# A two-layer graph block on one core: a unit's last sums stay in their PSUM banks, the edge weights are clipped on ScalarE, the maxima are spread in a line buffer

## The chip, the core and the metric

The kernel runs on one core of a Trainium2 chip. The metric is the device time in microseconds of one launch; the kernel before takes 1951.85 us (median of three runs, 1951.63 to 1953.33). One profiled execution has a span of 1949.7 us. The engines are named as in the profile: PE (TensorE, with PEld for its weight loads), DVE (VectorE), ACT (ScalarE), POOL (GpSimd) and SP (SyncE); the last two issue most of the DMAs here.

## The reference, cut to what matters

There are 4096 nodes with 512 features, and a symmetric pattern `adj` of 4096 x 4096 with positive weights on about 1.6% of the places.

```
# layer 0
x  = layernorm(x + relu(adj @ (max(sign(x), 0) @ sign(w0).T)))
# layer 1
node_att = softmax(x @ node_w, axis=0)
h = x @ edge_w
e = where(adj > 0, h @ h.T, -9e15)
out = (adj * node_att * softmax(e, axis=1)) @ (x @ w1) + bias
x  = layernorm(x + out)
```

## The kernel before, in words

The kernel has four stages in order of time.

1. 0 to about 950 us: layer 0. `adj` is split into two parts (`hi`, `lo`), and both are multiplied with the small integers of the other operand (L372, L373). The normalised rows go to DRAM, both as they are (`x1_d`) and in the combinations that later products need (`lop_d`).
2. `h`, transposed, in seven products for each 2 x 2 of blocks (`seven`, L100).
3. To about 1078 us: the scores. Blocks of 512 x 512 of `h @ h.T` are computed once each (`Single` L632, `Couple` L701) and turned for their mirror image (L602, L603). Each row block gets its mask and its row maximum on DVE (L564) and its sum of exponentials on ACT (L573). The raw scores go to DRAM (`s_d`).
4. From 1078 us to the end: the aggregation, which the change touches. It is a loop over 16 *units*, `Aggregate(g, r)` with g = 0..3 outside and r = 0..3 inside. A unit takes four score blocks: destinations g and g + 4, sources r and r + 4. DVE subtracts the row maximum (`shift`, L815), ACT takes the exponential (L816), and DVE multiplies by the edge weights, which are first clipped at zero (`weigh`, four instructions of 128 x 512 in L822). From the four blocks `r11, r12, r21, r22`, DVE makes the four combinations of a seven-product scheme in place (`combine`, L831 to L839: `t3`, then `t1`, `t2`, `t4`). PE multiplies seven pairs (index `m` in `main`): `m=0` is `r11`, 1 is `r21`, 2 is `r22`, 3 is `t4`, 4 is `t1`, 5 is `t2`, 6 is `t3`. Each product has two *halves* of one PSUM bank, four 128 x 512 matmuls in fp32, which the trace shows as eight passes (L991). A half is then read out of its bank into `total`, the sums over r: by an ACT copy at r = 0 (L995), by a DVE add at r > 0 (L997). From unit 2 to unit 14 product 0 is itself cut into seven smaller ones that are laid between the others (`second`, L932).

When the four units of one g are done, `todo` brings `join` (L1024) and `Finish`: a product with `w1` (L1079, read by DVE in L1090), the layernorm (L1120 to L1133), and the output.

What sets the order: one unit's `steps()`, the work that prepares the *next* unit (loads, masks, `shift`, `weigh`, `combine`), are dealt out evenly over the halves of the present one by `between`. Work of the first unit is `early_steps`, mixed into the end of stage 3. The tile framework then orders the instructions of each engine by its own estimates, so they can stand in another order than in the code; an engine takes its instructions in that order. Waits are on semaphores.

Buffers: `free` holds 6 + 7 tiles of 128 x 2048 (`slot`, `lent`), taken and given back in turn; `free_e` holds six lines of 128 x 512 (`line`); `rows` is a pool of four tiles of 128 x 512, which the `Finish` steps use for their rows `xb` (L1052, freed when the output DMA has read them) and `panel` for `spread`. Six PSUM banks go round in `next_bank`. `lopp` has four buffers for the left operands, loaded on SP's queue (L987).

`panel(A)` brings the row maxima of a destination group into a form in which they can be subtracted along the free axis: DVE spreads them (L775), PE transposes them (L781), ACT copies the result to a line (L785), which `shift` needs. It comes first in the work that a unit with r = 3 does for the next g.

Of the kernel before, what the change touches and what calls it, by code (L numbers as in the profile page):

```python
# [11 lines left out]
F32 = mybir.dt.float32  # L12
BF16 = mybir.dt.bfloat16
F32R = mybir.dt.float32r
AF = mybir.ActivationFunctionType
ALU = mybir.AluOpType
AX = mybir.AxisListType

P = 128
# [9 lines left out]
def kernel(  # L29
# [13 lines left out]
    nc = tc.nc  # L43
# [5 lines left out]
    BG = W // P  # L49
    HB = NB // 2  # L50
    HG = NG // 2
# [5 lines left out]
    rows = ctx.enter_context(tc.tile_pool(name="rows", bufs=4))  # L57
# [100 lines left out]
    with (  # L158
# [109 lines left out]
        ends = wp.tile([P, 2 * W], F32, name="ends", tag="ends")  # L268
# [74 lines left out]
        with tc.manual_schedule(engines={mybir.EngineType.DVE, mybir.EngineType.Activation}):  # L343
            for n in range(NB):
                b = n // 2 + n % 2 * HB
# [53 lines left out]
        more = [stream.tile([P, 2, 2 * W], F32, name="more", tag="stream") for _ in range(2)]  # L399
# [68 lines left out]
    free_e = deque(pan.tile([P, W], F32, name=f"line{n}", bufs=1) for n in range(6))  # L468
# [8 lines left out]
    def tick(force=False):  # L477
        now[0] += 1
        if turns and (turns[0][0] <= now[0] or force):
            turns.popleft()[1]()  # L480
        n = 1 + (len(stats) > 8)
        while stats and n and (stats[0][0]() <= now[0] or force):
            n -= stats[0][1]
            stats.popleft()[2]()
        for _ in range(1 + (len(exps) > 3)):
            if exps and (exps[0][0] <= now[0] or force):
                exps.popleft()[1]()

    def is_in(store, buf):
        return any(b is buf for b in store)  # L490

    def reclaim():

        for t, *hs in lent:
            if len(free_h) - 2 >= min(len(masks), 3) and all(is_in(free_h, h) for h in hs):
                for n in reversed(range(len(free_h))):
                    if is_in(hs, free_h[n]):
                        del free_h[n]
                free.append(t)

    def take(store=None):
        store = free if store is None else store
        while True:
            if closing[0] and store is free:
                reclaim()
            if store:
                break
            assert turns or stats or exps, (len(free), len(free_h), len(free_e), len(masks), now)
            tick(True)
        if closing[0] and store is free_h:  # L510
            for _, *hs in lent:
                if is_in(store, hs[0]) != is_in(store, hs[1]):
                    while not is_in(hs, store[0]):
                        store.rotate()
                    break
        return store.popleft()
# [236 lines left out]
    banks = deque()  # L753

    def next_bank():
        banks.rotate(-1)
        return banks[-1]
# [3 lines left out]
    def panel(A):  # L761

        cols = slice(A * BG, (A + 1) * BG)
        nm = small.tile([P, BG], F32, name="nm")
        nc.vector.tensor_reduce(nm, nmax_c[:, cols, :], AX.X, ALU.min)
        d = small.tile([P, BG, NG], F32, name="d")
        nc.vector.tensor_tensor(d, nm.unsqueeze(2).to_broadcast([P, BG, NG]), nmax_c[:, cols, :], ALU.subtract)
        nc.scalar.activation(d, d, AF.Exp)
        nc.vector.tensor_mul(d, d, sum_c[:, cols, :])
        f = pan.tile([P, BG], F32, name="f")  # L770
        nc.vector.tensor_reduce(f, d, AX.X, ALU.add)
        nc.vector.reciprocal(f, f)
        nc.vector.tensor_mul(f, f, node_att[:, cols])
        spread = rows.tile([P, BG, P], F32, name="spread", tag="rows")
        nc.vector.tensor_copy(spread, nm.unsqueeze(2).to_broadcast([P, BG, P]))  # L775
        if banks:
            pt = next_bank().rearrange("p (b w) -> p b w", w=P)
        else:
            pt = ps_tr.tile([P, BG, P], F32, name="ptm", tag="tr")
        for i in range(BG):  # L780
            nc.tensor.transpose(pt[:, i, :], spread[:, i, :], ident)  # L781
        if A % HG:
            free_e.append(panels[A - 1][1])
        mrow = take(free_e)
        nc.scalar.copy(mrow.rearrange("p (b w) -> p b w", w=P), pt)  # L785
        panels[A] = f, mrow


    pinned = [tc.keep_in_program_order]

    class Aggregate:
# [23 lines left out]
            pinned[0](nc.vector._custom_dve(TENSOR_ADD_SAT, out=q, in0=q, in1=m, s0=0.0, s1=-HUGE))  # L815
            nc.scalar.activation(q, q, AF.Exp)  # L816

        def weigh(self, n, then):
            q, a = self.q[n], self.a[n].rearrange("p b (c i) -> p b c i", i=P)
            for c in range(BG):  # L820
                qc = q[:, c, :].rearrange("p (b w) -> p b w", w=P)
                pinned[0](nc.vector.scalar_tensor_tensor(qc, a[:, :, c, :], 0.0, qc, ALU.max, ALU.mult))  # L822
            free.append(self.a[n])
            if then:
                self.mask(then)
# [15 lines left out]
        def steps(self, beside):  # L841

            self.q, self.a, self.since = [None] * 4, [None] * 4, [None] * 8

            def begin():
                for n in range(2):
                    self.load(n)
                    self.mask(n)
                if not beside:
                    self.load(2)  # L850
                    self.load(3)

            yield begin
            yield lambda: self.shift(0)
            yield lambda: self.shift(1)
            for n in range(2):
                yield lambda n=n: self.weigh(n, n + 2)
                yield lambda n=n: self.shift(n + 2)
            yield lambda: self.weigh(2, None)
            yield lambda: self.weigh(3, None)  # L860
            for n in range(4):
                yield lambda n=n: self.combine(n)

# [114 lines left out]
        def main(self, between, nxt=None, two=False):  # L978
            r11, t1, r21, r22 = self.q
            total = sums[:, self.g % 2]  # L980
            last = self.g == HG - 1 and self.r == HG - 1
            products, others = self.second(nxt) if two else ({}, {})
            turn = 0
            for m in (0, 1, 5, 6, 4, 2, 3) if last else (1, 2, 4, 6, 5, 3) if two else (0, 1, 2, 4, 6, 5, 3):
                rop = (lambda: r11, lambda: r21, lambda: r22, lambda: self.t4, lambda: t1, lambda: self.t2, lambda: self.t3)[m]()
                lop = lopp.tile([P, BG, HD], F32, name="lop")
                nc.sync.dma_start(lop, lop_d[self.r][:, m])  # L987
                for h in range(2):
                    ps = next_bank()
                    for c in range(BG):  # L990
                        nc.tensor.matmul(ps, lop[:, c, ts(h, P)], rop[:, c, :], start=(c == 0), stop=(c == BG - 1))  # L991
                    turn += 1
                    read = products[turn]() if turn in products else None
                    if self.r == 0:
                        nc.scalar.copy(total[:, m, h, :], ps)  # L995
                    else:
                        nc.vector.tensor_add(total[:, m, h, :], total[:, m, h, :], ps)  # L997
                    if read:
                        read()
                    between()  # L1000
                    if h:
                        free.append(rop)
                    for act in others.get(turn, ()):
                        act()
                if last:
                    for done in self.joins.get(m, ()):
                        join(self.g, done, nc.vector)

        joins = {1: (0,), 5: (1,), 6: (2,), 4: (3, 4), 2: (5,), 3: (6,)}

    def join(g, n, engine):

# [135 lines left out]
    def between():  # L1148
        tick()
        soon[0] = max(1, 2 - sum(m.t is not None for m in final))  # L1150
        while masks and len(free_h) > 2 and masks_h[0] < 8 and masks[0].unit <= unit[0] + 1:
            masks.popleft().load()
        for _ in range(2):
            if closing[0] and len(early_) > 2 and (len(early_) > 10 or now[0] % 2) and early_[0][0]():
                early_.popleft()[1]()
            if len(early_) < 10:
                break
# [61 lines left out]
    for n, u in enumerate(blocks):  # L1219
        nxt = blocks[n + 1] if n + 1 < len(blocks) else None  # L1220
        two = 2 <= n < len(blocks) - 1
# [5 lines left out]
        if nxt:  # L1227
            first.extend(nxt.steps(two))
            if n:
                first.popleft()()  # L1230
            if u.r == HG - 1:
                first.extendleft([lambda: panel(nxt.g + HG), lambda: panel(nxt.g)])
# [64 lines left out]
```

## Time and profile before

| engine | busy us | share of the span |
|---|---|---|
| PE | 1931.1 | 99% |
| DVE | 1438.0 | 74% |
| ACT | 694.8 | 36% |
| POOL | 300.1 | 15% |

In stage 4 the four costliest groups on DVE are the adds of L997 (148 of 680 ns, 100.6 us), the `shift` of L815 (2285 ns each for 128 x 2048), the `weigh` of L822 (684 ns each for 128 x 512) and the `combine` subtractions (2284 ns each). How to read it: a matmul row of 128 x 512 has a mean of 592 ns, but the passes overlap; in a run without waits a new pass starts each 429 ns (16 passes in 6.87 us in the chain of waits). The same holds for DVE, whose instructions start 0.60 us apart where one is listed with 0.68. Times in the timeline are microseconds from the span's start.

### The profile page before, as it was taken

What the parts mean: (1) busy time and instruction counts of PE and PEld (TensorE: products, weight loads), DVE (VectorE), ACT (ScalarE), POOL (GpSimd) and SP (SyncE); (2) the same over time, 40 slices, a digit from 0 to 9 for tenths busy, and PEclk for the clock granted to TensorE, in tenths of its full rate; (3) what the DMA queues carried; (4) which work ended last, traced back from release to release, by engine and by line L of the source; (5) the groups of instructions that cost most, each with busy time, mean ns of one, the idle gap of its engine ahead of it and who ended that gap; (6) DMA issues with size and microseconds to landing.
All of it is one profiled execution on the core that took longest, in us unless ns stands there. A gap on an engine that the chain in (4) does not pass through costs nothing.

```text
span 1949.7 us, 19192 instructions
## 1 busy us (share of the span) xinstructions
PE 1931.1 (99%) x6470; PEld 1153.5 (59%) x6470; DVE 1438.0 (74%) x2281; ACT 694.8 (36%) x1140; POOL 300.1 (15%) x424
## 2 busy tenths in 40 slices
PE   9999999999999999999999999999999999999998
PEld 6888888888644445455555444555555555555555
DVE  7766676676774576577565897898759987799757
ACT  5433333333213567577667420131303221231200
POOL 0122222122441111111121111110101110111000
PEclk9999999999999999999999999999999999999999
DMA  8888898888485578577679986776767766776731
GB/s 304 298 324 313 291 323 313 314 308 292 143 296 202 182 256 296 205 260 280 253 288 324 334 292 234 273 262 204 264 236 279 272 228 246 264 271 209 257 119 44
DMA packets 139010, 504.59 MB, mean 259 GB/s; under 512 B 14112, under 2 KB 14112, under 8 KB 131232
## 3 DMA queue, kind: packets, MB, share of 16 engines
q1 hardware_dynamic: 63648, 226.52, 34.0%
q0 software_dynamic: 66912, 247.49, 33.9%
q10 hardware_dynamic: 8352, 29.36, 4.2%
q8 instruction: 51, 0.84, 0.2%
q14 instruction: 47, 0.39, 0.1%
HBM read 381.68 MB, written 121.63 MB: 258 GB/s over the span
## 4 chain that ended last, share of the span: by engine, by line
PE 85%; DVE 5%; DMA 4%; issue 4%; ACT 1%; POOL 0%; SPq 0%; POOLq 0%; DVEq 0%; ACTq 0%
PE bank L991 29%; PE seven L701 12%; PE acc L373 11%; PE acc L372 11%; PE seven L100 5%; PE pe L632 4%; PE bank L932 3%; PE po L1079 3%; PE pt L602 2%; DMA s_d<-slot 2%; PE bank L1079 1%; PE acc L245 1%; PE pt L332 1%; PE pw L213 1%; ACT line L573 1%
## 5 line engine op out<-in xcount | busy, mean ns | idle before, releaser
L372 PE MATMUL acc<-xw,hi 128*128 128x512 f32 x960 | 376.4, 392 | 0.0
L373 PE MATMUL acc<-xw,lo 128*128 128x512 f32 x960 | 374.2, 390 | 0.0
L991 PE MATMUL bank<-lent,lop 128*128 128x512 f32 x800 | 356.2, 592 | 2.0 <-issue 1.4
L991 PE MATMUL bank<-slot,lop 128*128 128x512 f32 x784 | 349.6, 592 | 0.4 <-DMA lop<-lop_d 0.4
L991 PEld LDWEIGHTS bank<-lent,lop 128*128 128x128 f32 x800 | 151.6, 190 | 166.7 <-issue 160.8
L991 PEld LDWEIGHTS bank<-slot,lop 128*128 128x128 f32 x784 | 148.3, 190 | 161.2 <-issue 154.0
L364 DVE TENSOR_TENSOR lo<-at,hi 128x1024 fp32r<-128x1024 f32 x120 | 148.0, 1234 | 85.2 <-ACT hi L362 85.2
L373 PEld LDWEIGHTS acc<-xw,lo 128*128 128x128 f32 x960 | 180.3, 188 | 37.1 <-DVE lo L364 0.3
L372 PEld LDWEIGHTS acc<-xw,hi 128*128 128x128 f32 x960 | 180.2, 188 | 36.8
L362 ACT CAST hi<-at 128x1024 fp32r<-128x1024 f32 x120 | 126.4, 1054 | 203.4 <-PE acc L372 148.4
L997 DVE TENSOR_TENSOR over<-over,bank 128x512 f32<-128x512 f32 x148 | 100.6, 680 | 72.0 <-PE bank L991 71.9
L816 ACT ACTIVATE slot<-slot 128x2048 f32<-128x2048 f32 x37 | 70.7, 1911 | 182.0 <-DVE slot L815 160.6
L632 PE MATMUL pe<-hT 128*128 128x512 f32 (+3 forms) x384 | 132.1, 486 | 0.0
L564 DVE CUSTOM_DVE_ANT_0 line<-lent,slot 128x512 f32<-128x512 bf16 x144 | 93.0, 687 | 45.9 <-ACT slot L642 23.0
L573 ACT ACTIVATE line<-line,nmax_c 128x512 f32<-128x512 f32 x160 | 114.8, 724 | 22.2 <-DVE nmax_c L564 22.1
L816 ACT ACTIVATE lent<-lent 128x2048 f32<-128x2048 f32 x27 | 51.6, 1912 | 127.2 <-DVE lent L815 92.0
L701 PE MATMUL seven<-hT 128*128 128x512 f32 x192 | 89.8, 593 | 0.0
L815 DVE CUSTOM_DVE_ANT_1 slot<-slot,line 128x2048 f32<-128x2048 f32 x37 | 84.4, 2284 | 6.6 <-DMA slot<-s_d 5.7
L632 PEld LDWEIGHTS pe<-hT 128*128 128x128 f32 x384 | 64.6, 191 | 41.4 <-issue 33.8
L602 PEld LDWEIGHTS pt<-ident,lent 128*128 128x128 f32 x412 | 51.2, 141 | 53.0 <-issue 38.4
L1124 ACT ACTIVATE rstd<-mv,eps 128x1 f32<-128x1 f32 (+1 forms) x14 | 4.1, 296 | 213.6 <-DVE mv L1121 169.2
L603 ACT COPY slot<-pt 128x512 f32<-128x512 f32 (+3 forms) x126 | 69.5, 554 | 27.0 <-PE pt L602 23.2
(257 smaller groups left out, 2837.3 us busy)
## 6 DMA issues: line engine op xcount, KB each, us to landing
at<-in_adj_t_dram SPq DMA_DIRECT2D x60, 1024.0 KB, 6.6
lop<-lop_d SPq DMA_DIRECT2D x99, 512.0 KB, 4.8
slot<-s_d POOLq DMA_DIRECT2D x37, 1024.0 KB, 7.1
lent<-in_adj_t_dram POOLq DMA_DIRECT2D x37, 1024.0 KB, 7.5
s_d<-slot POOLq DMA_DIRECT2D x33, 1024.0 KB, 7.2
slot<-in_adj_t_dram POOLq DMA_DIRECT2D x27, 1024.0 KB, 7.3
lent<-s_d POOLq DMA_DIRECT2D x27, 1024.0 KB, 7.3
lent<-in_adj_dram SPq DMA_DIRECT2D x48, 512.0 KB, 5.3
```

What stands on the lines that cost most here:

```text
L100: nc.tensor.matmul(banks[bank][q], lop(m, q)[k], rop(m)[k], start=(first and k == 0), stop=(k == K - 1), skip_group_check=not first,)
L362: nc.scalar.copy(hi, aq)
L364: nc.vector.tensor_sub(lo, aq, hi.bitcast(F32))
L372: nc.tensor.matmul(acc, hi[:, c, :], xw[:, kb, :], start=(kb == 0), stop=False)
L373: nc.tensor.matmul(acc, lo[:, c, :], xw[:, kb, :], start=False, stop=(kb == NB - 1))
L564: nc.vector.tensor_tensor_reduce(line, mask, src, -1.0, HUGE, ALU.add, ALU.min, accum_out=nmax_c[:, b, c : c + 1])
L573: nc.scalar.activation(line, line, AF.Exp, bias=nmax_c[:, b, c : c + 1], scale=-1.0, accum_out=sum_c[:, b, c : c + 1])
L632: nc.tensor.matmul(pe[:, lo * P :], hT[:, k, ts(A * BG + i, P)], hT[:, k, (B * BG + lo) * P : (B + 1) * W], start=(k == 0), stop=(k == KD ...
L701: nc.tensor.matmul(ps, left[m][:, k, q, :], right[m][:, k, :], start=(first and k == 0), stop=(k == KD // 2 - 1), skip_group_check=not first,)
L816: nc.scalar.activation(q, q, AF.Exp)
L991: nc.tensor.matmul(ps, lop[:, c, ts(h, P)], rop[:, c, :], start=(c == 0), stop=(c == BG - 1))
L997: nc.vector.tensor_add(total[:, m, h, :], total[:, m, h, :], ps)
```

## The change: what it does and what it is for

There are four edits in stage 4.

- **Held sums.** A unit with r < 3 doesn't read out the last of its products; the two banks stay open (`held`), and the next unit begins with the same `m` and adds onto them. So that both share an `m`, the order of the products becomes 2, (0), 4, 6, 5, 3, 1 at even r and 1, (0), 4, 6, 5, 3, 2 at odd r. This is to save DVE adds.
- **Clip on ScalarE.** `max(a, 0)` leaves `weigh`: ACT applies a Relu to the weights in place (`clip`), and DVE multiplies all 128 x 2048 in one instruction. The first unit keeps the old form.
- **Spread in a line.** In stage 4 `spread` is taken from `free_e` rather than from the pool that `Finish` uses.
- The steps of a unit are laid anew so that each `clip` stands ahead of its `weigh`.

```diff
 def panel(A):
-        spread = rows.tile([P, BG, P], F32, name="spread", tag="rows")
+        if banks:
+            line = take(free_e)
+            spread = line.rearrange("p (b w) -> p b w", w=P)
+        else:
+            spread = rows.tile([P, BG, P], F32, name="spread", tag="rows")
...
         nc.scalar.copy(mrow.rearrange("p (b w) -> p b w", w=P), pt)
+        if banks:
+            free_e.append(line)
...
+        def clip(self, n):
+            nc.scalar.activation(self.a[n], self.a[n], AF.Relu)
+
-        def weigh(self, n, then):
+        def weigh(self, n, then, clipped=False):
             q, a = self.q[n], self.a[n].rearrange("p b (c i) -> p b c i", i=P)
-            for c in range(BG):
-                qc = q[:, c, :].rearrange("p (b w) -> p b w", w=P)
-                pinned[0](nc.vector.scalar_tensor_tensor(qc, a[:, :, c, :], 0.0, qc, ALU.max, ALU.mult))
+            if clipped:
+                q = q.rearrange("p c (b w) -> p c b w", w=P)
+                nc.vector.tensor_mul(q, q, a.rearrange("p b c w -> p c b w"))
+            else:
+                for c in range(BG):
+                    qc = q[:, c, :].rearrange("p (b w) -> p b w", w=P)
+                    pinned[0](nc.vector.scalar_tensor_tensor(qc, a[:, :, c, :], 0.0, qc, ALU.max, ALU.mult))
...
             yield lambda: self.shift(0)
-            yield lambda: self.shift(1)
-            for n in range(2):
-                yield lambda n=n: self.weigh(n, n + 2)
-                yield lambda n=n: self.shift(n + 2)
-            yield lambda: self.weigh(2, None)
-            yield lambda: self.weigh(3, None)
+            yield lambda: (self.shift(1), self.clip(0))
+            yield lambda: (self.weigh(0, 2, True), self.clip(1))
+            yield lambda: self.shift(2)
+            yield lambda: self.weigh(1, 3, True)
+            yield lambda: (self.shift(3), self.clip(2))
+            yield lambda: (self.weigh(2, None, True), self.clip(3))
+            yield lambda: self.weigh(3, None, True)
...
-            for m in (0, 1, 5, 6, 4, 2, 3) if last else (1, 2, 4, 6, 5, 3) if two else (0, 1, 2, 4, 6, 5, 3):
+            ends = (1, 2) if self.r % 2 else (2, 1)
+            order = (1, 0, 5, 6, 4, 2, 3) if last else (ends[0], *(() if two else (0,)), 4, 6, 5, 3, ends[1])
+            for m in order:
...
-                    ps = next_bank()
+                    more = bool(self.r) and m == order[0]
+                    keep = self.r < HG - 1 and m == order[-1]
+                    ps = Aggregate.held.pop(0) if more else next_bank()
...
-                    if self.r == 0:
+                    if keep:
+                        Aggregate.held.append(ps)
+                    elif self.r == 0 or more and self.r == 1:
                         nc.scalar.copy(total[:, m, h, :], ps)
                     else:
                         nc.vector.tensor_add(total[:, m, h, :], total[:, m, h, :], ps)
...
+        held = []
-        joins = {1: (0,), 5: (1,), 6: (2,), 4: (3, 4), 2: (5,), 3: (6,)}
+        joins = {0: (0,), 5: (1,), 6: (2,), 4: (3, 4), 2: (5,), 3: (6,)}
```

More of the change, by code (lines that the diff above doesn't have):

```diff
@@ L988, in main @@
                 for h in range(2):
-                    ps = next_bank()
+                    more = bool(self.r) and m == order[0]
+                    keep = self.r < HG - 1 and m == order[-1]
+                    ps = Aggregate.held.pop(0) if more else next_bank()
                     for c in range(BG):
-                        nc.tensor.matmul(ps, lop[:, c, ts(h, P)], rop[:, c, :], start=(c == 0), stop=(c == BG - 1))
+                        nc.tensor.matmul(
+                            ps,
+                            lop[:, c, ts(h, P)],
+                            rop[:, c, :],
+                            start=(not more and c == 0),
+                            stop=(not keep and c == BG - 1),
+                        )
                     turn += 1
                     read = products[turn]() if turn in products else None
-                    if self.r == 0:
+                    if keep:
+                        Aggregate.held.append(ps)
+                    elif self.r == 0 or more and self.r == 1:
                         nc.scalar.copy(total[:, m, h, :], ps)
```

## The prediction

> **What bounds the kernel now.** I read the page first, then PE's waits in stage 4, then single stretches of the timelines of PE, DVE and ACT.
>
> ```profile
> span 1949.7 us, 19192 instructions
> ...
> PE 1931.1 (99%) x6470; PEld 1153.5 (59%) x6470; DVE 1438.0 (74%) x2281; ACT 694.8 (36%) x1140; POOL 300.1 (15%) x424
> ```
>
> PE is the bound, and the change takes no matmul away: the passes of L991 (1584), L932 (364) and L1079 (448) stay what they are. So DVE time that is saved counts only where PE waits for DVE. How much is that in stage 4?
>
> ```profile
> PE po L1079 <- DVE left L1065: 2.4, 2, 1.2
> PE bank L991 <- issue: 1.4, 2, 0.7
> PE bank L991 <- DMA lop<-lop_d: 1.0, 2, 0.6
> ```
>
> The ends of matmuls are modelled, so these sums are somewhat too small. From the starts in PE's timeline:
>
> ```profile
> 1527.01 1.03 PE L1079 MATMUL bank<-over 128*128 128x256 f32 x4
> 1529.24 1.13 PE L1079 MATMUL po<-over,left 128*128 128x256 f32 x4 [1.20 <-DVE left L1065]
> ```
>
> Four passes of 0.216 us end at 1527.87, so the next was 1.37 late, and its first passes cost another 0.1: 1.5. Done in this way for all of stage 4, the late starts are 0.7 (at 1402.8, `lop` load), 0.2 (1473.6), 0.9 (1485.7), 1.5 (1529.2), 0.2 (1682 to 1685), 0.9 (1702.4), 1.5 (1745.9) and 0.9 (1837.1, `lop`): 6.8 us in all. That is the most the change can bring, 0.35% of the time.
>
> Where do they come from? In the timeline of DVE, at the end of g = 1:
>
> ```profile
> 1458.13 0.69 DVE L997 TENSOR_TENSOR over<-over,bank 128x512 f32<-128x512 f32 x1 [1.17 <-PE bank L991]
> 1460.01 0.43 DVE L775 COPY spread<-nm 128x512 f32<-128x512 f32 x1 [1.19 <-ACT xb L1133]
> ...
> 1462.17 0.63 DVE L775 COPY spread<-nm 128x512 f32<-128x512 f32 x1
> ...
> 1463.48 2.29 DVE L815 CUSTOM_DVE_ANT_1 slot<-slot,line 128x2048 f32<-128x2048 f32 x1 [0.23 <-ACT line L785]
> ```
>
> Unit 7 began at 1431.3, yet its first `shift` starts at 1463.5: `spread` had to wait until `Finish` let go of `rows`. Until then DVE idles 1 to 3 us before each add; after that it has a whole unit's preparation in 22 us, and is 99% busy from 1480 to 1530 (49.36 of 50 us). The lateness at 1485.7 and 1529.2, and likewise at 1702.4 and 1745.9 for g = 2, is this jam.
>
> [...]
>
> **The change part by part.**
>
> *Held sums.* Per g, the add of the last product goes away at r = 1 and 2, and the first add of r = 1 becomes an ACT copy in exchange for the one that r = 0 saves: 6 DVE adds, 24 in all, at 0.60 us apart 14.4 us of DVE. No PE time. The order of products costs something, see below.
>
> *One multiplication.* Four instructions 0.60 apart (2.41) become one of 2.28, 2.20 apart: 0.21 us saved, 60 times (15 units of 4): 12.6 us of DVE. The units beside which they stand have DVE slack, apart from the jam.
>
> *Clip.* 60 times 1.83 to 1.91 us, 110 to 115 us on ACT, which is idle most of stage 4 (9.6 of 50 us busy from 1130 to 1180). Beside PE it costs nothing in general, since six banks go round and a read-out may come some 15 us late. But `clip` adds a wait for a DMA on ACT's queue, with everything behind it waiting too. In the built order of instructions there is one place where PE is close behind: the first `clip`, of the second unit's first weights, stands at the end of stage 3, between L603 of the last full block and the last diagonal block's copies:
>
> ```profile
> 1074.01 0.59 ACT L603 COPY lent<-pt 128x512 f32<-128x512 f32 x1 [1.14 <-PE pt L602]
> 1075.36 0.72 ACT L573 ACTIVATE line<-line,nmax_c 128x512 f32<-128x512 f32 x1 [0.77 <-DVE nmax_c L564]
> ...
> 1076.08 0.46 ACT L642 COPY lent<-pe 128x384 f32<-128x384 f32 x1
> ```
>
> Those weights were issued at 1070.0 and took 6.0 us (the view of L809), so `clip` runs 1076.1 to 1077.9; L573 and the 384-wide copy follow at 1077.9 and 1078.65. PE transposes that copy:
>
> ```profile
> 1076.83 0.49 PE L602 MATMUL pt<-ident,lent 128*128 128x128 f32 x3
> 1077.15 1.06 PE L632 MATMUL pe<-hT 128*128 128x128 f32 x8
> ```
>
> Now it can start at 1079.25, 2.4 us late; the last use of `hT` ends 2.4 later, and with it the start of the `w1` load that overwrites it.
>
> *Order of products in unit 0.* Before, `t1` is the fourth product; now it is the third. The scheduler puts two of the eight 128 x 512 matmuls of `t3` ahead of it, but those need `combine(0)`.
>
> ```profile
> 1087.86 0.69 DVE L1234 TENSOR_TENSOR line<-over 128x512 f32<-128x512 f32 x1 [4.32 <-DMA over<-in_w_dram]
> ...
> 1089.99 2.49 DVE L822 SCALAR_TENSOR_TENSOR slot<-slot,slot 128x512 f32<-128x512 f32 x4
> ...
> 1093.00 2.28 DVE L831 TENSOR_TENSOR lent<-lent,slot 128x2048 f32<-128x2048 f32 x1
> 1095.32 2.29 DVE L833 TENSOR_TENSOR slot<-slot,slot 128x2048 f32<-128x2048 f32 x1
> ```
> ```profile
> 1092.11 7.03 PE L991 MATMUL bank<-lent,lop 128*128 128x512 f32 x16
> 1098.98 1.45 PE L991 MATMUL bank<-slot,lop 128*128 128x512 f32 x3
> ```
>
> DVE waits for `w1` (L1234) with the last `weigh` and the combinations behind it: `t3` is made at 1095.3 and `t1` at 1097.6, in time for the fourth product at 1098.98. In the new order of DVE a `spread` (0.4), two small panel instructions and the fourth `w1` subtraction come ahead of the `weigh` as well: about 0.5 more, `t3` at 1095.8 and `t1` at 1098.1. PE wants `t3` at 1092.1 and stalls 3.8; two matmuls (four passes, 1.7) later it wants `t1` at 1097.6 and stalls 0.6: 4.4 us. With the `w1` load 2.4 later, `t1` comes 2.4 later too. PE's own 2.4 us at the diagonal block is inside this wait, so the sum is 4.4 + 2.4 = 6.8 us. The lower end is 4.4 (the weights land earlier), the upper about 8.5 (the smaller copies behind, too).
>
> *Spread in a line.* At units 7 and 11 `shift` can begin some 25 us earlier: the scores had landed by 1425.2 and the weights by 1434.8, and no `xb` is in the way. The jam goes; DVE's new order even has `left` ahead of the last two `weigh`s. I count 0.9 + 1.5 + 0.2, twice, as gone: 5.1 us (the 0.2 at 1473.6 with them). PE now meets the transposes L781 in a unit's first product, where the second `spread` is just made: 0.1 to 0.2 each, three times, 0.4 in all.
>
> *`lop` loads.* On SP's queue one more `lop` load now stands ahead of the outputs and `xb` loads that held it back at 1402.8 and 1837.1, so 0.7 + 0.9 = 1.6 should go. I take 1.4.
>
> *Clips in later units* come 2 us ahead of `weigh` or make DVE wait as long (weights landing, Exp, clip in a row); before, `t1` was ready 10 to 20 us ahead of its product except in units 0, 8 and 12, so this is hidden by those margins.
>
> Sum: + 6.8 + 0.4 - 5.1 - 1.4 = + 0.7 us, 1951.85 + 0.7 = 1952.5. The 27 us of DVE that the change saves are worth nothing by themselves.
>
> **Rivals.**
> - *Faster.* The jam and the late loads go, and unit 0 costs next to nothing, since weights and `w1` land early. Then - 6.8 + 0.4 = 1945.5. Against it: DVE's 4.32 us of idling before L1234 shows that `w1` comes last there, and nothing speeds it up. With the lower end of 4.4 the result is 1949.9, which is no change.
> - *Slower.* Clip's waits make new stalls: DVE waits in a unit for weights + clip, with L997 and L1090 behind it, `po` has only two banks, and in the joining units DVE was at 99%. If half of the 6.5 us stays and two units lose 2 us more: 1951.85 + 6.8 + 0.4 - 3.2 + 4 = 1959.8; with only the first, 1955.9. For it: `t1` is wanted one product (7 to 8.6 us) earlier in all units. Against it: in unit 4, which joins too but whose `spread` was free, PE loses nothing.
>
> **How the numbers follow.** My case 0.62, slower 0.28, faster 0.10. The range from 1948.5 to 1957.5 takes in the lower end at unit 0 with all gains (1949.9 less a little) and the first form of the slower rival. The borders of "no change" are 1947.9 and 1955.8; the chances are those of the cases.
>
> **What would show it.** Right: in the new profile PE's late starts after 1200 have shrunk from 6.8 to under 1.5 us; there is a gap before L602 near 1077, and one of 3 to 5 us before the third product of unit 0; the first `shift` of unit 8's blocks starts within 10 us of unit 7's start; DVE is 25 to 30 us less busy and ACT 110 more. Wrong: no gap in unit 0 (then faster), or new waits of L991 or L1079 on DVE or ACT in units 8 to 9 and 12 to 13 (then slower).

## The result, and the profile after

The changed kernel takes 1957.68 us (median of 6 runs) where the kernel before takes 1952.34 (6 runs, measured together): a ratio of 1.0028, 95% interval 1.0015 to 1.0041. It is slower by 2.9 to 8.0 us. The forecast was 1952.5 with a range up to 1957.5, and "slower" had 0.28.

Line numbers shift with every edit. The main products are L991 before, L1010 in the changed kernel and L994 to L1014 in the others; the smaller products are L932 before and L946 after, the read-out of a main product L997 and L1024, of a smaller one L947 and L961. PE's transposes in `panel` are L781 and L785, the spread ahead of them L775 and L779. On DVE `shift` is L815 and L821, `weigh` L822 and L831 (in four instructions L835), `t3` and `t1` are made in L831 and L833, after the change in L844 and L846; `clip` on ACT is L825.

The page of the changed kernel, the same lines as before:

```profile
span 1956.4 us, 19088 instructions
...
PE 1934.1 (99%) x6470; PEld 1154.9 (59%) x6470; DVE 1409.5 (72%) x2077; ACT 803.9 (41%) x1200; POOL 300.0 (15%) x424
```

DVE is 28.5 us less busy and ACT 109 us more, as the parts of the change say (25 to 30 and 110 were forecast). The clip of 128 x 2048 takes 1.91 us on ACT (60 of L825, mean 1907 ns), as the Exp of that size does (L816, 1911 ns), and no ACT_TABLE_LOAD (1.28 us) belongs to L825: the trace has 14, as before. PE has 3 us more, with the same number of passes.

PE's waits from 1060 us to the end (columns: engine and line, waited for, us in total, times, longest):

```profile
PE bank L785 <- DVE line L779: 2.2, 1, 2.2
PE bank L946 <- DVE over L961: 1.9, 1, 1.9
PE pt L602 <- ACT lent L642: 1.3, 1, 1.3
PE bank L1010 <- issue: 0.8, 1, 0.8
PE bank L1010 <- DVE slot L846: 0.3, 1, 0.3
```

None of the three waits of before is left: no `left`, no `lop`, and the one put down to `issue` is another one, in unit 0. In their place stand these five. Taken from the starts in PE's timeline, as the prediction did it, stage 4 has 9.9 us of late starts after the change and 6.8 before. They are:

- 1.7 at 1082 to 1084, L602 behind the clip on ACT, at the end of stage 3
- 1.7 at 1098 to 1101, the third product of unit 0 (`t3`, then `t1`)
- 2.4 at 1235, the transposes of the second panel (L785)
- 3.8 at 1356 to 1361, L946 in unit 5, 1.7 of it passes at half speed after the gap (0.853 us apart where 0.429 is usual; the granted clock is 0.50 from 1357.9 to 1361.3)
- 0.3 in small pieces

The clip that holds up L602 waits for its weights, and the copy that L602 needs stands behind it on ACT. The last pass of the product that it copies (L632) starts on PE at 1077.8, the copy not until 1082.06:

```profile
1079.54 1.92 ACT L825 ACTIVATE lent<-lent 128x2048 f32<-128x2048 f32 x1 [1.91 <-DMA lent<-in_adj_t_dram]
1081.36 0.70 ACT L573 ACTIVATE line<-line,nmax_c 128x512 f32<-128x512 f32 x1
...
1082.06 0.46 ACT L642 COPY lent<-pe 128x384 f32<-128x384 f32 x1
```

The time from the start of the last matmul to the end is 0.4 longer too (7.0, now 7.4). With the 3.1 us by which the late starts have grown that makes 3.5 us, inside the interval.

The spans of the two traces differ by more, 6.7 us. The rest came before unit 0: a wait of L100 at 575 us, and passes at half speed near 1038 (0.853 us apart, granted clock 0.50 from 1037.1 to 1040.5). (The stages lie earlier than the description of the kernel has them: L372 and L373 of layer 0 run from 58 to 507 us, L100 from 508 to 605, the scores from 605 on.) Up to some 1017 us the order of instructions on every engine is the same but for `xb` loads on SP that came forward to 990. The last experiment tells whether that part belongs to the change.

### The profile page after: what moved, and what is told of

Read it like the earlier page. It is cut to its first block, busy times and chain, and to the rows that moved or that the text cites. A ratio compares the mean times of both kernels' runs of the same rounds, so it can differ in the third digit from the quotient of the medians.

```text
span 1956.4 us, 19088 instructions
## 1 busy us (share of the span) xinstructions
PE 1934.1 (99%) x6470; PEld 1154.9 (59%) x6470; DVE 1409.5 (72%) x2077; ACT 803.9 (41%) x1200; POOL 300.0 (15%) x424
## 4 chain that ended last, share of the span: by engine, by line
PE 88%; DMA 5%; issue 3%; DVE 3%; ACT 1%; POOL 1%; POOLq 0%; DVEq 0%; SPq 0%; ACTq 0%
PE bank L1010 32%; PE seven L701 12%; PE acc L373 11%; PE acc L372 11%; PE pe L632 4%; PE bank L946 4%; PE seven L100 4%; PE po L1107 3%; PE pt L602 2%; DMA s_d<-slot 2%; PE bank L1107 1%; PE acc L245 1%; PE pw L213 1%; PE pt L332 1%; ACT line L573 1%
## 5 line engine op out<-in xcount | busy, mean ns | idle before, releaser
L372 PE MATMUL acc<-xw,hi 128*128 128x512 f32 x960 | 376.4, 392 | 0.0
L373 PE MATMUL acc<-xw,lo 128*128 128x512 f32 x960 | 374.2, 390 | 0.0
L1010 PE MATMUL bank<-slot,lop 128*128 128x512 f32 x832 | 371.5, 594 | 0.3 <-DVE slot L846 0.3
L1010 PE MATMUL bank<-lent,lop 128*128 128x512 f32 x752 | 334.1, 592 | 0.8 <-issue 0.8
L1010 PEld LDWEIGHTS bank<-slot,lop 128*128 128x128 f32 x832 | 158.4, 191 | 169.7 <-issue 164.2
L1010 PEld LDWEIGHTS bank<-lent,lop 128*128 128x128 f32 x752 | 142.6, 190 | 155.7 <-issue 151.6
L373 PEld LDWEIGHTS acc<-xw,lo 128*128 128x128 f32 x960 | 180.3, 188 | 37.1 <-DVE lo L364 0.3
L372 PEld LDWEIGHTS acc<-xw,hi 128*128 128x128 f32 x960 | 180.2, 188 | 36.8
L632 PE MATMUL pe<-hT 128*128 128x512 f32 (+3 forms) x384 | 133.7, 491 | 0.0
L1024 DVE TENSOR_TENSOR over<-over,bank 128x512 f32<-128x512 f32 x124 | 84.1, 679 | 53.7 <-PE bank L1010 53.4
L825 ACT ACTIVATE lent<-lent 128x2048 f32<-128x2048 f32 x39 | 74.3, 1907 | 114.1 <-DMA lent<-in_adj_t_dram 109.1
L822 ACT ACTIVATE lent<-lent 128x2048 f32<-128x2048 f32 x33 | 63.1, 1911 | 122.1 <-DVE lent L821 114.3
L822 ACT ACTIVATE slot<-slot 128x2048 f32<-128x2048 f32 x31 | 59.2, 1909 | 108.8 <-DVE slot L821 108.8
L821 DVE CUSTOM_DVE_ANT_1 lent<-lent,line 128x2048 f32<-128x2048 f32 x33 | 75.3, 2285 | 28.9 <-DMA lent<-s_d 28.7
L632 PEld LDWEIGHTS pe<-hT 128*128 128x128 f32 x384 | 65.3, 192 | 42.4 <-issue 34.8
L821 DVE CUSTOM_DVE_ANT_1 slot<-slot,line 128x2048 f32<-128x2048 f32 x31 | 70.9, 2286 | 24.3 <-DMA slot<-s_d 24.2
L602 PEld LDWEIGHTS pt<-ident,lent 128*128 128x128 f32 x412 | 51.1, 141 | 55.3 <-issue 38.1
```

Of the source, the lines that this page charges most:

```text
L372: nc.tensor.matmul(acc, hi[:, c, :], xw[:, kb, :], start=(kb == 0), stop=False)
L373: nc.tensor.matmul(acc, lo[:, c, :], xw[:, kb, :], start=False, stop=(kb == NB - 1))
L602: nc.tensor.transpose(pt[:, j, :], src[:, ts(j, P)], ident)
L632: nc.tensor.matmul(pe[:, lo * P :], hT[:, k, ts(A * BG + i, P)], hT[:, k, (B * BG + lo) * P : (B + 1) * W], start=(k == 0), stop=(k == KD ...
```

## The experiments

The kernel before and the twelve others in one table. "Late" is the sum of late starts of PE from 1060 us to the end in that kernel's trace, so it leaves out what happens in the stages that the change does not touch. The ratio is to the kernel before in the same comparison.

| kernel | held | clip | spread | w1 behind | ratio (95% interval) | late, us |
|---|---|---|---|---|---|---|
| before, two traces | | | rows | | 1 | 6.8; 6.3 |
| line | | | short | | 0.9996 (0.9988 to 1.0004) | 4.0 |
| line_inplace | | | in place | | 0.9987 (0.9978 to 0.9996) | 7.2 |
| best_noheld | | | in place | yes | 0.9981 (0.9973 to 0.9988) | 2.5 |
| clip | | yes | rows | | 1.0010 (1.0003 to 1.0016) | 10.9 |
| held | yes | | rows | | 1.0046 (1.0034 to 1.0058) | 15.1 |
| held_w1 | yes | | rows | yes | 1.0017 (1.0010 to 1.0023) | 9.4 |
| held_line | yes | | short | | 1.0031 (1.0020 to 1.0042) | 10.6 |
| best | yes | | in place | yes | 0.9973 (0.9962 to 0.9984) | 2.2 |
| the change | yes | yes | short | | 1.0028 (1.0015 to 1.0041) | 9.9 |
| after_w1 | yes | yes | short | yes | 1.0019 (1.0012 to 1.0025) | 5.8 |
| after_two_plain | yes | 13 of 15 units | short | yes | 0.9996 (0.9987 to 1.0005) | 4.9 |
| best_clip | yes | yes | in place | yes | 1.0004 (0.9995 to 1.0012) | 5.4 |

"w1 behind" keeps the subtractions on `w1` behind unit 0's combinations, and "in place" spreads the maxima in the buffer that takes the transposed row afterwards; both are explained below. One trace is one execution, and the runs of one kernel lie 4 to 10 us apart, so "late" and ratio need not agree to the microsecond.

### The three parts alone

The theory after the result: the clip costs (A). The rival: the order of products costs (B). Each part went into the kernel before by itself, and the clip was taken out of the changed kernel.

The short buffer alone (`line`):

```diff
-        spread = rows.tile([P, BG, P], F32, name="spread", tag="rows")
+        if banks:
+            line = take(free_e)
+            spread = line.rearrange("p (b w) -> p b w", w=P)
...
+        if banks:
+            free_e.append(line)
```

> The kernel before with the short spread buffer alone. My theory (the jam at units 7 to 8 and 11 to 12 comes from the spread that waits for Finish's rows): the late starts near 1485, 1529, 1702 and 1746 go, 5.1 us, and the transposes cost 0.4 to 2.4: 2.5 to 4.7 us faster than before, near 1948.5. Rival (the short buffer itself makes the wait of 2.2 us at L785 in the first product of a panel unit, three times): no change or slower, 1952 to 1956.

No difference that can be measured (0.9996; 2.5 to 4.7 us had been expected), and in the trace both statements came true. The jam is gone: near 1485, 1529, 1702 and 1746 nothing over 0.25 remains. But there is a new gap at L785. The waits of PE:

```profile
PE bank L785 <- DVE line L779: 1.7, 1, 1.7
PE bank L997 <- DMA lop<-lop_d: 1.0, 2, 0.5
```

The clip and the one multiplication alone (`clip`; edit: `clip`, `weigh(..., True)` and the new order of steps from the diff, nothing else):

> The kernel before with the clip on ScalarE and the single multiplication alone. Theory A (the clip is what costs: it holds ACT's queue at the end of stage 3, and makes the weigh, the mask loads and the scores loads behind them later): 3 to 6 us slower than before, 1955 to 1958, with a late start before L602 near 1077. Theory B (the order of the products costs): within 1 us of before or up to 2 us faster, since DVE is 12.6 us less busy.

1.0010: 0.6 to 3.1 us slower, less than theory A said, but not what B said either. L602 waits 2.2 us for the copy behind the clip, at 1081, and a late small product stands in unit 5 too (1.4 us at 1350, L940), here without held sums:

```profile
PE pt L602 <- ACT lent L642: 2.2, 1, 2.2
PE bank L940 <- DVE over L955: 1.9, 3, 1.2
PE po L1087 <- DVE left L1073: 1.5, 2, 0.8
PE po L1087 <- DVE xb L1098: 1.1, 2, 0.9
```

Held sums and their order alone (`held`; edit: `order`, `ends`, `more`, `keep`, `held` and `joins` from the diff):

> The kernel before with the held sums and their order of products alone. Theory A (clip costs): within 2 us of before, the only late start it adds is the one before the third product of unit 0, 2 to 4 us, and the late lop loads go, 1.5 us. Theory B (the order costs, since t1 is wanted a product earlier): 3 to 6 us slower than before, with late starts of L991 or L932 on DVE in several units.

1.0046, 6.6 to 11.3 us slower: the order costs more than the clip, so far B. Yet not "in several units": 6.8 of it are in unit 0. Its timeline on PE:

```profile
1089.44 4.46 PE L996 MATMUL bank<-slot,lop 128*128 128x512 f32 x10
1097.31 2.04 PE L996 MATMUL bank<-lent,lop 128*128 128x512 f32 x2 [3.41 <-issue]
1099.59 6.73 PE L996 MATMUL bank<-slot,lop 128*128 128x512 f32 x11 [0.23 <-DVE slot L833]
```

The third product starts 3.6 us late, and `t1` makes PE wait once more. Then something that no step of the prediction had: two passes of `t3` and the first ones of `t1` take longer than 0.43. The windows around it (columns: stretch, us, busy time of PE, PEld, DVE, ACT, POOL with the number of instructions, granted PE clock, DMA share, GB/s):

```profile
1090.00:1093.00 3.00, 3.00 (x9) 1.33 (x8) 2.86 (x5) 0.58 (x1) 0.00 (x0) 1.00 0.98 344
1093.00:1097.00 4.00, 0.90 (x3) 0.07 (x1) 4.00 (x5) 0.58 (x1) 2.24 (x3) 0.91 0.71 197
1099.60:1104.00 4.40, 4.40 (x6) 1.87 (x7) 4.37 (x2) 0.00 (x0) 1.50 (x2) 0.60 1.02 387
1104.00:1108.00 4.00, 4.00 (x11) 1.84 (x10) 4.00 (x3) 2.12 (x2) 0.00 (x0) 1.00 1.02 385
```

After the gap the clock is 0.60 on average for 4.4 us. The waiting itself cost 4.0 us (3.6, and 0.4 for `t1`, which DVE has ready at 1099.53), close to the 4.4 that the prediction had for the order of products; the slow passes made it 6.8.

The changed kernel without the clip (`held_line`; edit: `weigh` and the steps as before):

> The changed kernel without the clip: weights multiplied in four instructions as before, held sums and short spread buffer kept. Theory A (clip costs): 1 to 4 us faster than before, 1948 to 1951, no gap near 1077 and no late L946 in unit 5. Theory B (the order costs): as the changed kernel, 1956 to 1959.

1.0031, no better than the changed kernel with its clip. Theory A alone is out: the order of unit 0 costs 7.0 here. But A's gaps are in fact absent when the clip is: nothing at 1082, and nothing in unit 5, where the change loses 3.8. So two costs are in play, and with the clip the cost of unit 0 is smaller (1.7). Why is that?

### Who is late in unit 0

On DVE the last `weigh` and the combinations stand behind the subtractions on `w1`. In the changed kernel:

```profile
1090.03 0.69 DVE L1262 TENSOR_TENSOR line<-over 128x512 f32<-128x512 f32 x1 [1.22 <-DMA over<-in_w_dram]
...
1093.03 2.49 DVE L835 SCALAR_TENSOR_TENSOR slot<-slot,slot 128x512 f32<-128x512 f32 x4
...
1095.55 2.29 DVE L844 TENSOR_TENSOR lent<-lent,slot 128x2048 f32<-128x2048 f32 x1
1097.88 2.29 DVE L846 TENSOR_TENSOR slot<-slot,slot 128x2048 f32<-128x2048 f32 x1
```

`w1` lands at 1089.9. In held_line it lands at 1090.2, though unit 0 started there 2.3 us earlier on PE (1080.5, with the change 1082.8). The load is issued at 1081.27, which is 1.3 us before the late L602: its last reader on PE, L632, stands ahead of that L602, not behind. So the clip delays PE and not `w1`; PE comes later to a wait that ends at the same time.

To test it, the four subtractions are kept behind what was traced before them on DVE, so behind the combinations (held_w1, after_w1):

```diff
-            todo.append(lambda: nc.vector.tensor_sub(t3, r22, r12))
+            todo.append(lambda: tc.keep_in_program_order(nc.vector.tensor_sub(t3, r22, r12)))
...
```

> Held sums and their order alone, with the four subtractions on w1 kept behind unit 0's combinations on DVE. Theory A (unit 0's stall is the wait for the w1 load, which stands in DVE's queue ahead of the last weigh and the combinations): the gap before the third product, 6.8 us with its slow passes after it, is gone, t3 is made near 1092 and t1 near 1094; 6 to 8 us faster than held sums alone, within 2 us of before. Theory B (the order itself wants t1 too early, w1 or not): the gap shrinks by less than half, and it stays 5 us or more slower than before.

The gap of 6.8 is 0.8, and the ratio goes from 1.0046 to 1.0017, with intervals that don't meet. It is the wait for `w1`. The kernel stays 2.0 to 4.5 us slower than before, where theory A had at most 2; in its trace the jam, the late `lop` load at 1841 and the longer last stretch are left. DVE starts the last `weigh` at 1087.5, before the load is in:

```profile
1087.51 2.50 DVE L822 SCALAR_TENSOR_TENSOR slot<-slot,slot 128x512 f32<-128x512 f32 x4 [1.98 <-ACT slot L816]
1090.09 2.29 DVE L831 TENSOR_TENSOR lent<-lent,slot 128x2048 f32<-128x2048 f32 x1
1092.42 2.29 DVE L833 TENSOR_TENSOR slot<-slot,slot 128x2048 f32<-128x2048 f32 x1
```

> The changed kernel with the same four subtractions kept behind the combinations. Theory A (the 1.5 us by which the first clip holds PE at the last diagonal block was hidden in the wait for w1, and comes out when that goes): the 1.6 us before the third product go, the gap near 1082 stays at 1.5 to 2.3, so 1 to 2.5 us faster than the changed kernel, still 2 to 4 us slower than before. Rival (clip does not matter): as the kernel before or faster, 1949 to 1953.

The trace is as theory A said: 1.7 before the third product became 0.6, and 1.1 stays at L602. The time is 1.0019 against 1.0028, which two intervals that overlap can't tell apart.

### The second panel

> The short spread buffer alone, but the maxima are spread in the buffer that takes the transposed row afterwards, so that the second panel's spread need not wait for the first one's transposes. My theory: the gap of 1.9 us before L785 near 1228 goes to under 0.3; 1.5 to 2 us faster than the short buffer alone, 2.5 to 4 faster than before. Rival (the second spread is late because DVE waits for the lop load ahead of it): the gap stays.

Seen against the short buffer alone:

```diff
+        if A % HG:
+            free_e.append(panels[A - 1][1])
+        mrow = take(free_e)
         if banks:
-            line = take(free_e)
-            spread = line.rearrange("p (b w) -> p b w", w=P)
+            spread = mrow.rearrange("p (b w) -> p b w", w=P)
...
```

The gap is gone, and with 0.9987 it is faster than before by 0.8 to 4.3 us; against the short buffer alone the intervals overlap. The rival was half right about the order of events, as DVE of the changed kernel shows:

```profile
1232.85 0.43 DVE L929 TENSOR_TENSOR slot<-slot 128x256 f32<-128x256 f32 x1 [7.03 <-DMA slot<-lop_d]
...
1234.32 0.68 DVE L1024 TENSOR_TENSOR over<-over,bank 128x512 f32<-128x512 f32 x1
1234.92 0.42 DVE L779 COPY line<-nm 128x512 f32<-128x512 f32 x1
```

The one spare buffer is read by the first panel's transposes up to 1232.3, so the second spread could not stand ahead of the four combinations for the smaller products (L929 to L932), and so came behind their wait for a load. With a buffer each, all eight transposes run at once, at 1228.96 in `best` (1.04 us from the first to the end of the last), and the wait does not matter.

This run had a late `w1` of its own: it landed 13.0 us after its issue (in the trace of before 9.5). The old order of unit 0 then lost 4.4 us at its fourth product, 1.8 of it slow passes. So the margin at `w1` was thin before the change too.

### The clip in unit 5, and at the end of stage 3

In the changed kernel, unit 5 starts at 1328.67. ACT at its start, POOL's queue while it prepares unit 6, then DVE and PE:

```profile
1326.74 1.91 ACT L822 ACTIVATE lent<-lent 128x2048 f32<-128x2048 f32 x1 [1.26 <-DVE lent L821]
1328.56 1.89 ACT L825 ACTIVATE lent<-lent 128x2048 f32<-128x2048 f32 x1
1330.35 1.89 ACT L825 ACTIVATE slot<-slot 128x2048 f32<-128x2048 f32 x1
```

```profile
1333.07 0.75 POOL L815 DMA_DIRECT2D lent<-in_adj_t_dram  x1 [12.64 <-DVE lent L831]
1336.67 0.76 POOL L815 DMA_DIRECT2D slot<-in_adj_t_dram  x1 [2.85 <-DVE lent L831]
1337.42 0.75 POOL L808 DMA_DIRECT2D lent<-s_d  x1
```
```profile
1349.54 2.29 DVE L821 CUSTOM_DVE_ANT_1 lent<-lent,line 128x2048 f32<-128x2048 f32 x1 [7.95 <-DMA lent<-s_d]
...
1353.09 0.65 DVE L1024 TENSOR_TENSOR over<-over,bank 128x512 f32<-128x512 f32 x1
1353.81 2.29 DVE L831 TENSOR_TENSOR lent<-lent,lent 128x2048 f32<-128x2048 f32 x1
1356.02 0.41 DVE L961 TENSOR_TENSOR over<-over,bank 128x256 f32<-128x256 f32 x1
```
```profile
1356.48 1.13 PE L946 MATMUL bank<-slot,slot 128*128 128x256 f32 x4 [1.87 <-DVE over L961]
```

Two clips and an Exp in a row on ACT make the second `weigh` (L831) end 7.7 us into the unit (before: 4.9), so the second mask load goes out right ahead of the load of scores. The scores take some 12 us, the shift waits 7.95 us at the head of DVE's queue, and the read-out L961 behind it comes 1.9 us late for PE. Such a load of 1 MB took 12.1, 11.7 and 12.0 us where it was issued 0.75 us behind the mask load (the change, after_w1, best_clip), and 7.4 and 7.7 where it was issued 3.3 and 3.2 us behind it (before, after_two_plain). Whether the order in POOL's queue or the sharing of the DMA engines makes the difference, no run tells apart.

The test takes the clip from two of the fifteen units, unit 1 (whose first clip stands at the end of stage 3) and unit 6:

```diff
+        plain = ((0, 1), (1, 2))
+
         def clip(self, n):
+            if (self.g, self.r) in Aggregate.plain:
+                return
...
-            if clipped:
+            if clipped and (self.g, self.r) not in Aggregate.plain:
```

> The changed kernel with the w1 subtractions pinned, where two of the fifteen clipped units are weighed in four instructions as before, without clip: unit 1 and unit 6. My theory: the gap before L602 near 1082 goes (1.1 in the run with the clips), since no clip stands in ACT's queue there, and so does the late L946 of unit 5 near 1354 (1.6), since the weighs end sooner and the mask loads go out before the scores' loads; the other gaps (L785 near 1234) stay. Rival (DMA timing of the held order makes the late L946): it stays above 1 us.

Both gaps go. POOL and DVE in that run, where unit 5 starts at 1325.91:

```profile
1331.19 0.76 POOL L815 DMA_DIRECT2D slot<-in_adj_t_dram  x1 [2.05 <-DVE lent L839]
1334.35 0.75 POOL L808 DMA_DIRECT2D lent<-s_d  x1 [2.40 <-issue]
```
```profile
1342.03 2.29 DVE L821 CUSTOM_DVE_ANT_1 lent<-lent,line 128x2048 f32<-128x2048 f32 x1 [3.20 <-DMA lent<-s_d]
```

The scores are issued 8.4 us into the unit instead of 8.8, hardly sooner; but the mask load is 3.2 us ahead of them and not 0.75, and the shift starts 16.1 us into the unit and not 20.9. The ratio is 0.9996 against 1.0019, intervals apart: 0.0023 of the time, 4.5 us, for the clips of two units. In this trace other gaps of 0.4 to 0.9 us stand in unit 4 and near 1740, so its sum of late starts is only 0.9 smaller: the traces show the two gaps go, but not where the whole 4.5 us comes from. (The trace of after_w1 is of an execution 2.5 us faster than that kernel's median.) How the 4.5 us divide between the two units was not tried.

> The changed kernel with both repairs: the w1 subtractions behind unit 0's combinations, and the maxima spread in place. It differs from the best so far (0.9973 of before) in the clip alone. My theory (clip's waits on ACT cost, its 12.6 us of DVE bring nothing): the gap before L602 near 1082 and the late L946 near 1355 are there, 2 to 5 us slower than the best, 1951 to 1955. Rival (clip is neutral once the other two are repaired): within 1 us of the best, 1948 to 1950.

1.0004 against 0.9973 for the same kernel without the clip: 0.0031, some 6 us, intervals apart. The trace shows 3.2 us more of late starts, at L602 (1.3) and in unit 5 (1.8). The clip costs. Between held_line and the change it was not seen, because PE, late at L602 already, loses 3.6 us less in unit 0 (3.4 with L602, where held_line has 7.0): it waits less for the late `w1`, and no slow passes follow. That is about what unit 5 loses. The clip was always tried together with the one multiplication, so that the loss is the clip's and not the multiplication's is argued from the waits on ACT, not shown apart.

### What is left when the stalls are taken out

> Held sums, spread in place, w1 subtractions behind unit 0's combinations, and no clip. If the stalls seen so far are what counts: neither the gap before the third product (7.0) nor the one at L785 (2.0) of held sums with the short buffer is left, nor the jam of before (5.1): 8 to 10 us faster than held sums with the short buffer, 3 to 5 us faster than before, 1948 to 1950. If the saved stalls come back elsewhere: within 2 us of before.

0.9973, 3.1 to 7.4 us faster than before, and faster than the changed kernel. All that PE waits for after 1060 us:

```profile
PE bank L999 <- DVE slot L836: 0.5, 1, 0.5
PE bank L999 <- DMA lop<-lop_d: 0.5, 1, 0.5
PE bank L935 <- DVE over L950: 0.3, 1, 0.3
```

> The kernel before with the spread in place and the w1 subtractions pinned behind unit 0's combinations, without held sums and without clip. My theory (held sums bring PE nothing; their order costs only through w1): within 1.5 us of the best, 1948 to 1951. Rival (the held order is what brings the gain, by its earlier lop loads): 2 to 4 us slower than the best.

0.9981. It can't be told from `best`: the held sums, which take 14.5 us of DVE away (1436.2 to 1421.7), bring nothing that is measured. The gain is the spread in place and the subtractions moved; how it divides is open, since the spread in place alone has 0.9987.

### The stages ahead of the change

> The kernel before once more, for a second trace of it. If the gaps that differ ahead of the changed part (L100 near 575, L602 near 933, slow passes near 1038) come and go by chance, at least one of them differs by over 0.5 us from the first trace of the same kernel; if they belong to the kernels with held sums, none of them does.

A second trace of the kernel before has a span of 1956.6, where the first has 1949.7. It shows all three: L100 near 576 is 2.3 us late with 1.8 of slow passes, L602 near 938 is 2.5 late with 1.6, and slow passes stand near 1043. PE's waits from 500 to 1060 us in that second trace:

```profile
PE pt L602 <- DVE lent L746: 2.3, 1, 2.3
PE seven L100 <- DVE hT L121: 2.2, 1, 2.2
PE ptm L781 <- ACT slot L603: 1.7, 1, 1.7
PE pt L602 <- ACT lent L642: 1.2, 1, 1.2
```

From unit 0 to the end, both traces of before take the same (871.4 and 871.1 us; the changed kernel's takes 873.6, to which its late L602 ahead of unit 0 comes). So these gaps come and go in one and the same kernel, and two spans alone say little about a change of 0.3%.

## Why the prediction was wrong

Most of its places were right, and it was wrong on three sizes: one was too large and made up in part for two that were too small. By its own steps, in late starts:

- *Spread in a line*, - 5.1: right. None of the jam's late starts is left in the changed kernel. The first shift beside unit 7 starts at 1448.3, 4.8 us after that unit's start (32 before).
- *`lop` loads*, - 1.4: right, 1.6 went.
- *Held sums* and *One multiplication*, no PE time: right; 28.5 us less DVE bought nothing.
- *Order of products in unit 0* with the clip, + 6.8: it was 3.4. Alone the order cost 4.0 in waits, where 4.4 was forecast, and 2.8 in slow passes on top, which no step had; that these too make 6.8 is chance. The failing sentence is "With the `w1` load 2.4 later, `t1` comes 2.4 later too": the load does not wait for the clip, so PE's late L602 (1.7) and its wait for `t3` (1.7) share one end. They overlap instead of adding up.
- *Panels*, + 0.4: it was 2.4. The step took it that the second spread "is just made" when PE comes to it; it has to wait for the first one's transposes, and then stood behind the combinations for the smaller products and their load.
- *Clips in later units*, "hidden by those margins": this is the step that failed. The margin was measured on `t1`, but the wait did not reach PE by `t1`. It went over a freed slot to a mask load, to the scores behind it, to a shift, and to the read-out behind that: 3.8 us in unit 5, 1.7 of it slow passes. Without this cost the late starts would have been below those of before (9.9 less 3.8 is 6.1). In the time, the clip costs some 6 us (best_clip against best), L602 included.

By the signs it named, L602's gap, the early `shift` and the busy times of DVE and ACT came true; but unit 0's gap is 1.7 and not 3 to 5, and after 1200 us the late starts are 6.5 and not under 1.5.

From 7.5 us of late starts (6.8 and the forecast 0.7): - 3.4 at unit 0, + 2.0 at the panel, + 4.1 at the clips and small pieces, - 0.3 at jam and `lop` make 9.9. The tail's 0.4 comes on top.

The rival "slower" described this: DVE waits in a unit, "with L997 and L1090 behind it". Its size, 1955.9 to 1959.8, was right, but it looked for the waits in units 8 to 9 and 12 to 13, and they came in unit 5; in that its size was in part luck. Its place in the argument was too small, because the case for it was a margin looked up on one path.

What stays open: why `w1` takes 13.0 us once and 8.3 to 9.8 otherwise, and what makes the early gaps at L100 and L602 come and go (for the slow passes near 1038 see the last section). The last stretch is 0.4 to 0.5 longer in every trace with held sums, `held` alone too, and in none without; how they lengthen it was not looked into.

## What to carry to other kernels

Before you call a delay hidden, follow the buffer that the delayed instruction frees: which load waits for it, what is queued next to that load, and which instruction at the head of an engine's queue waits for the data. Two delays that end at the same event don't add (here 1.7 us at L602 and 1.7 before `t3`); and taking one away may show the other (unit 0 costs 7.0 us in held_line, without the clip, and 1.7 with it). With PE 99% busy, 14.5 us saved on DVE (`best` against `best_noheld`) bought nothing that is measured, and the end of a wait did (0.0029 from `held` to `held_w1`); look for what stands at the head of a queue without being urgent, like the `w1` subtractions here.

## What was not expected of the hardware

Some gaps on PE cost more than themselves here. From 510 to 1930 us, the 14 traces hold 14 late starts of 2.0 us or more. Behind 9 of them passes ran at half rate (0.853 us where 0.429 is usual) and cost 1.6 to 1.8 us more, in held and held_line 2.8 and 3.0; five of 2.05 to 2.40 had none. Slow passes came behind shorter gaps too: between 1034 and 1042 us all 14 traces have one of 1.8 us, mostly with shorter ones just ahead, and in 9 traces slow passes follow.

The granted clock shows it too. In that time it is either 1.00 or 0.50, and each fall lasts 3.41 us (in held and held_line 6.83). In the trace of the change the falls start at 1037.07, at 1357.93 and, at the end of the last products, at 1951.84 us: 320.85 and 914.77 us after the first, which is 94.0 and 268.0 times 3.413. Two pairs of stretches of that length, columns as above: the first of before_again, with two gaps of 1.4 and 1.8 us; the second of the change, with the gap of 2.40 at L785. In the first pair PE is busy for 1.17 of 3.42 us and the clock of the next stretch is 0.50; in the second it is busy for 1.52 of 3.41 us and the next stretch is at 1.00:

```profile
1037.21:1040.63 3.42, 1.17 (x6) 0.42 (x4) 1.55 (x10) 2.39 (x8) 0.00 (x0) 1.00 1.01 412
1040.63:1044.04 3.41, 2.75 (x7) 1.73 (x8) 1.27 (x5) 2.64 (x9) 1.61 (x3) 0.50 0.73 220
```
```profile
1231.63:1235.04 3.41, 1.52 (x7) 0.63 (x5) 2.16 (x6) 2.38 (x2) 0.00 (x0) 1.00 0.14 58
1235.04:1238.46 3.42, 3.07 (x11) 1.64 (x12) 3.42 (x3) 1.48 (x2) 0.00 (x0) 1.00 0.37 153
```

What decides whether the clock falls behind a gap was not shown.
